# Adding twelve tiles of layer 0's expert outputs, where six were, beside its last four blocks

## The chip, the cores and the metric

The kernel runs on one core of a Trainium2 chip, as one launch. The metric is the device time of that core in microseconds (us). TensorE (PE) multiplies, PEld is its weight load, VectorE (DVE) does elementwise work and statistics, ScalarE (ACT) the activation functions and copies, GpSimd (POOL) the scatters with indices, and SyncE (SP) issues most of the loads.

## The reference: two layers of graph aggregation and experts

There are 3327 nodes with 256 features, `x`, and a sparse weighted adjacency `adj`. Each of two layers does the following, with a layernorm without parameters, `ln`, ahead of each half:

```
layer 0   x = x + relu(adj @ (ln(x) @ W) + b)
          x = x + sum over the 2 best of 8 experts, weighted:
                  relu(ln(x) @ W1[e] + b1[e]) @ W2[e] + b2[e]      (hidden size 1024)
layer 1   A = tanh(max(adj,0)^2)  kept to the 700 largest of each row
          x = x + relu(A @ (tanh(ln(x) @ Wp + bp) @ Wg) + bg)
          x = x + ln(x) + sum over the 2 best of 8 experts, weighted: (hidden size 256, gelu)
```

In both layers the two experts of a node are those with the largest scores of a linear router on `ln(x)`, and their weights are a softmax over the two scores. All arithmetic is in 32-bit floats. In the inputs no row of `adj` has more than 700 positive entries, so nothing is dropped in layer 1.

## The kernel before: tiles, panels, blocks, and the passage between the layers

**Tiles and panels.** The nodes are padded to 3328, which is 26 tiles of 128. `x` and a second array of the same size, `s`, stay in SBUF as 26 tiles of 256 columns. An aggregation (`aggregate`, line 326) goes through 13 panels of 256 nodes; for each panel two chunks of the adjacency are loaded into a ring of six places of 128x3328 numbers (`ring`, line 124), and TensorE multiplies them with all 26 tiles of `s` (line 340). `s` is only read there, so it is free while the experts run.

**Blocks.** The router lists each node's features under its two experts in `xlist0` in HBM. An expert's rows are then worked off in blocks of 256 rows (`experts`, line 700). One `step` (line 858) loads a later block's tokens, weights and biases through SP (lines 752 to 774, five loads, into two places of the ring, up to three blocks ahead), transposes the next block's tokens (line 785, copied by DVE in line 788), runs the first product (line 797, activation in line 804) and the second (line 839), adds the bias and multiplies by the weight on DVE (lines 846 and 847), and scatters the rows to their nodes' places in `ys0` in HBM with two indirect stores of GpSimd (line 464). A node has two rows in `ys0`, one for each of its experts.

**The order of the blocks.** `late_order` (line 68) writes it out by hand. Layer 0 has 30 blocks that always run, steps 0 to 29: the first eight are full blocks that could be planned before the last panels were there, and four single blocks of 128 rows are mixed in (steps 12, 17, 22 and 27). The planning goes in tiers: the first block of every expert, then the second of every expert, then the rest. After step 7 the first tier has been scattered, after step 16 (`tiers_done`, line 882) the second as well.

**What is done early.** The outputs of the first tiles can be added to `x` before the last blocks are done, if all rows of these tiles lie in blocks that have been scattered. The function `usual` (line 632) counts the rows of the first tiles for each expert, compares them with the rows that the blocks cover, and gives a flag; all engines branch on it in line 1179. In the first arm, `load_outputs` (line 901, SP) brings `ys0` rows of the first `BEGUN` tiles into columns of `s`, `add_loaded` (line 913, DVE) adds a tile's two rows to `x`, and `statistics` (line 246, DVE) takes mean and variance and works out the reciprocal root in three Newton steps. The one block's tokens that are transposed across the branch are put into `s` too (the `place` of line 1025). In the other arm all of that comes after the last block.

**The passage between the layers** (`between`, line 1090). `turned_pairs` (line 1053) goes through groups of tiles, `FOURS`. For a group that was not begun it loads the outputs into ring place 5 or 4 in turn (line 902), adds them (line 916) and takes statistics (lines 254 to 266); then, for each pair of tiles, it normalizes (line 276, into one of three buffers `xn`), transposes (line 288) and copies (line 289). `second_features` (line 1073) multiplies by `Wp` (line 1079), takes tanh (line 1086, `h2T`), multiplies by `Wg` (line 296) and copies the result into `s` (line 299). The loads of outputs of the groups not begun wait for all scatters. The first two panels of layer 1's matrix are filtered here as well (`filter_behind`, line 1113): DVE takes the maximum with 0 (line 1117), ScalarE the square and tanh in four pieces (lines 1120 and 1121). The first of these chunks stands on DVE behind the normalization of the last group but one, the others behind that of the last group. Then `aggregate` starts for layer 1.

**What sets the order.** [...] A scheduler places the instructions by its own estimates and priorities; `behind` (line 204) and `issue_after` pin an instruction behind another one.

Of the kernel before, what the change touches and what calls it, by code (L numbers as in the profile page):

```python
# [10 lines left out]
F32 = mybir.dt.float32  # L11
BF16 = mybir.dt.bfloat16
I32 = mybir.dt.int32
# [9 lines left out]
P = 128  # L23
NT = 26
NP = NT * P
D = 256
DC = D // P
E = 8
# [7 lines left out]
TOPK = 700  # L36
# [3 lines left out]
K = 2  # L40
# [18 lines left out]
EARLY = 8  # L59
# [5 lines left out]
FIXED = (4, 6)  # L65
# [9 lines left out]
    return order + list(range(LATE_PAIRS + fixed, LATE))  # L75


BEGUN, FIRST_TILES = 6, 14
FREE_PAN = NPAN - RING // NCHUNK
assert K * EARLY_PAN * PW >= E * (SB - 1) + EARLY * SB  # L80
PAIRS = [(t, 2) for t in range(0, NT, 2)]
FOURS = [(0, 2)] + [(t, 4) for t in range(2, NT, 4)]


@with_exitstack
def gnn_moe_two_layers(
# [24 lines left out]
    nc = tc.nc  # L111
# [3 lines left out]
    work = ctx.enter_context(tc.tile_pool(name="work", bufs=3))  # L115
# [5 lines left out]
    x = state.tile([P, NT, D], F32, name="x")  # L121
# [5 lines left out]
    for t in range(0, NT, 4):  # L127
        n = min(4, NT - t)
# [13 lines left out]
        out=before,  # L142
        in_=before,
# [53 lines left out]
    rows_written, early_rows, outputs, last_product, last_y = [], [], [], [], []  # L197
# [6 lines left out]
    def behind(instructions):  # L204

        if instructions and any(i is instructions[-1].ins for i in nc.cur_bb.bb.instructions):
            return tc.issue_after(instructions[-1].ins)
        return nullcontext()
# [37 lines left out]
    def statistics(t0, n, kept=None):  # L246


        st = work.tile([P, n, 6], F32, name="ln_st")
        mv, guess = kept or (  # L250
            work.tile([P, n, 2], F32, name="ln_mv"), work.tile([P, n], I32, name="ln_guess")
        )
        for g in range(n):
            nc.vector.bn_stats(out=st[:, g, :], in_=x[:, t0 + g, :])  # L254
            nc.vector.bn_aggr(out=mv[:, g, :], in_=st[:, g, :])
        ve = work.tile([P, n], F32, name="ln_ve")
        nc.vector.tensor_scalar(ve, mv[:, :, 1], EPS, None, ALU.add)  # L257
        half = work.tile([P, n], I32, name="ln_half")
        nc.vector.tensor_scalar(half, ve.bitcast(I32), 1, None, ALU.logical_shift_right)
        nc.vector.tensor_scalar(guess, half, -1.0, float(0x5F3759DF), ALU.mult, ALU.add)  # L260
        rs = guess.bitcast(F32)
        nw = work.tile([P, n], F32, name="ln_nw")
        for _ in range(3):
            nc.vector.scalar_tensor_tensor(nw, rs, -0.5, rs, ALU.mult, ALU.mult)
            nc.vector.tensor_tensor(nw, nw, ve, ALU.mult)
            nc.vector.scalar_tensor_tensor(rs, nw, 1.5, rs, ALU.add, ALU.mult)
        return mv, rs
# [83 lines left out]
    def rows_of(a, t0, n):  # L351
        return a[t0 * P : (t0 + n) * P, :].rearrange("(n p) d -> p n d", p=P)
# [279 lines left out]
    def usual(tiles, rows_, small):  # L632


        cnt = tokens(tiles, "pl_first_cnt")
        nc.vector.tensor_tensor(cnt, cnt, rows_, ALU.is_gt)
        most = work.tile([P, 1], F32, name="pl_most", bufs=1)
        nc.vector.tensor_reduce(most, cnt, AX.X, ALU.max)
        nc.vector.tensor_scalar(most, most, -1.0, 1.0, ALU.mult, ALU.add)
        for number, limit in small:  # L640
            nc.vector.scalar_tensor_tensor(
                most[0:1, :], number, float(limit), most[0:1, :], ALU.is_le, ALU.mult
            )
        flag = work.tile([P, 1], I32, name="pl_flag", bufs=1)
        nc.vector.tensor_copy(flag, most)
        return nc.values_load(flag[0:1, 0:1], min_val=0, max_val=1)
# [266 lines left out]
    def add_loaded(yt, t0, n):  # L913
        x_t = x[:, t0 : t0 + n, :]
        for k in range(K):
            nc.vector.tensor_tensor(x_t, x_t, yt[:, :, k * D : (k + 1) * D], ALU.add)  # L916
# [40 lines left out]
    def count(pan, chunks):  # L957
# [9 lines left out]
    layer0 = experts(  # L967
        xlist0, ys0, "0", FIXED[0], H, AF.Relu, f0_w1T, f0_b1, f0_w2T, f0_b2,
        nc.vector.tensor_copy,
    )  # L970
# [27 lines left out]
    with tc.issue_after(last_product[0].ins):  # L998
# [13 lines left out]
    most_all = const.tile([1, 1], F32, name="most_all")  # L1012
# [4 lines left out]
    most_int = const.tile([1, 1], I32, name="most_int")  # L1017
    nc.vector.tensor_copy(most_int, most_all)
    late = plan(positive.rearrange("p n i k -> p (n i k)"))
    layer0.steps_to(late, EARLY)  # L1020
    written = list(outputs)
    layer0.steps_to(late, layer0.always - 4)
    in_s = s.rearrange("p n d -> p (n d)")
    at = BEGUN * K * D
    layer0.step(late, place=in_s[:, at : at + DC * SB].rearrange("p (c b) -> p c b", c=DC))
# [3 lines left out]


    first_usual = usual(
        BEGUN, late[4][:, 0:E], [(late[5][0:1, :], FIXED[0]), (most_all, TOPK + 0.5)]
    )
    before_branch, rows_before = layer0.state(), list(rows_written)
    begun_stats = (
        const.tile([P, BEGUN, 2], F32, name="begun_mv"), const.tile([P, BEGUN], I32, name="begun_rs")
    )
    begun = []
    for t, n in FOURS:
        if t < BEGUN:  # L1040
            yt = in_s[:, 0 : n * K * D] if not begun else in_s[:, 2 * K * D : (2 + n) * K * D]
            begun.append((yt.rearrange("p (n d) -> p n d", n=n), t, n))

    def begin():
        for b in begun:
            add_loaded(*b)
        return statistics(0, BEGUN, begun_stats)


    ahead = RING // NCHUNK - 1  # L1050
# [2 lines left out]
    def turned_pairs():  # L1053


        for i, (t0, n0) in enumerate(FOURS):

# [67 lines left out]
    def new_layer1():  # L1125
        return experts(
            xlist1, ys1, "1", FIXED[1], D, AF.Gelu, f1_w1, f1_b1, f1_w2, f1_b2,
            nc.scalar.copy, kept=(EARLY // 2, w2_all, gate),
        )
# [47 lines left out]
            nc.scalar.dma_start(out=rows_of(out, t, n), in_=x[:, t : t + n, :])  # L1177

    with tc.If(first_usual > 0) as arms:
        layer0.step(late)  # L1180
        output_loads.clear()
        for yt, t, n in begun:
            load_outputs(yt, ys0, t, n, written, "read0")
        layer0.step(late)
        with behind(last_y):
            begin()
        layer0.steps_to(late, layer0.always)
        between()
        layer1 = new_layer1()
        aggregate(gnn_b_sb, filter_chunk, panels1(layer1), loaded=ahead)  # L1190
        late1 = first_blocks(layer1)


        layer1.steps_to(late1, layer1.tiers_done)
        written = list(outputs)
        layer1.step(late1, place=blk.tile([P, DC, SB], F32, name="xT_arms", bufs=1))
        second_usual = usual(FIRST_TILES, late1[4][:, E:], [(late1[5][0:1, :], FIXED[1])])
        before_inner = layer1.state()
        with tc.If(second_usual > 0) as inner:
            first_tiles = [(t, 2) for t in range(0, FIRST_TILES, 2)]  # L1200
            yts = [
                ring[i % RING][:, PIECE - 2 * K * D :].rearrange("p (n d) -> p n d", n=2)
                for i in range(len(first_tiles))
            ]
            k = 0
            while len(layer1.started) < layer1.always:
                layer1.step(late1)
                if k < len(first_tiles):
                    load_outputs(yts[k], ys1, *first_tiles[k], written, "read1")
                with behind(last_y):  # L1210
                    if 0 <= k - 2 < len(first_tiles):
                        add_loaded(yts[k - 2], *first_tiles[k - 2])
                if 0 <= k - 3 < len(first_tiles):
                    t, n = first_tiles[k - 3]
                    nc.sync.dma_start(out=rows_of(out, t, n), in_=x[:, t : t + n, :])
                k += 1
            assert k - 3 >= len(first_tiles)
            finish([(t, 2) for t in range(FIRST_TILES, NT, 2)])
        with inner.Else():
            layer1.back_to(before_inner)  # L1220
            layer1.rest(late1)
            finish(FOURS)
    with arms.Else():
        layer0.back_to(before_branch)
        rows_written[:] = rows_before
        layer0.rest(late)
        output_loads.clear()
        for yt, t, n in begun:
            load_outputs(yt, ys0, t, n, outputs)
        begin()  # L1230
        between()
        layer1 = new_layer1()
        most_reg = nc.values_load(most_int[0:1, 0:1], min_val=0, max_val=NP * GROUP)
        with tc.If(most_reg > TOPK) as many:
            with tc.tile_pool(name="topk", bufs=1) as tk:
                topk_rows(tc, tk, ring, psy, pst, adj, s, x, gnn_b_sb, ident, filtered, add_relu)
            for pan in range(NPAN):
                panels1(layer1)(pan)
        with many.Else():

            layer1.loaded.clear()
            first_arm = list(rows_written)
            rows_written.clear()
            aggregate(gnn_b_sb, filter_chunk, panels1(layer1), loaded=ahead)
        rows_written.extend(first_arm)
        early_rows.extend(first_arm)
        layer1.rest(first_blocks(layer1))
        finish(FOURS)

# [140 lines left out]
```

## Time and profile before

| what | value |
|---|---|
| median of 3 runs | 1262.3 us (1259.44 to 1262.47) |
| the profiled execution | 1255.26 us |
| its span in the trace | 1253.5 us |
| granted TensorE clock, mean | 0.989 |
| busy: PE / PEld / DVE / ACT / POOL | 96% / 83% / 57% / 41% / 23% |
| layer 0's aggregation ends, layer 1's starts | about 340 us, 805 us |
| layer 0's last four blocks, steps 26 to 29 | start 694.2, 708.2, 716.1 and 730.4 us, end 744.2 us |
| layer 1's aggregation ends | about 1099 us |

Times within the execution are counted from the start of its span. The profile's rows name an engine, a line of the code, the operation and the tiles that it writes and reads, with a count; a number in brackets is how long the engine sat idle before it, and what ended that. A matmul of 32-bit floats with 256 columns appears as two records. "SPq" is the queue in which SP issues its loads. Matmul rows in a timeline [...]overlap a little; the chain of waits gives the time from issue to issue.

### The profile page before, as it was taken

Reading aid. Unit: us, or ns where it says so; the run is one execution under the profiler, and the core shown is the slowest. Engines: PE = TensorE matmul, PEld = TensorE weight load, DVE = VectorE, ACT = ScalarE, POOL = GpSimd, SP = SyncE. Lnnn points to the kernel's source line nnn. Section 1 sums busy time; section 2 is a strip of 40 time slices with the busy share of each in tenths; the row PEclk is TensorE's granted clock in tenths of the full one; section 3 lists DMA queues with packets and bytes.
Section 4 is the critical chain, followed back from the end, with each engine's and each line's share of the span. In section 5 each row is a group of like instructions: output and inputs, shape, how many; then the busy total and the mean of one; then the engine's idle time right before and its main releaser. Section 6 shows DMA issues by size and latency. Waiting matters only on the chain.

```text
span 1253.5 us, 18523 instructions
## 1 busy us (share of the span) xinstructions
PE 1201.3 (96%) x5816; PEld 1035.3 (83%) x5816; DVE 712.2 (57%) x2919; ACT 519.3 (41%) x963; POOL 289.7 (23%) x363
## 2 busy tenths in 40 slices
PE   6999999999999999999999998999999999999992
PEld 5888888888888888888888887788888888877771
DVE  8267767677663111111111148668999998784454
ACT  3797455541022222323232234995455552043330
POOL 2023122131231111111111110302323223264432
PEclk9999999999999999999999998999999999999996
DMA  9676554454267655757566557244445542477696
GB/s 365 170 248 215 181 181 165 160 198 139 63 228 238 207 178 177 257 173 247 186 224 210 181 203 266 94 164 166 168 171 198 179 147 82 130 243 220 204 272 213
DMA packets 119546, 241.60 MB, mean 193 GB/s; under 512 B 21568, under 2 KB 89936, under 8 KB 112400
## 3 DMA queue, kind: packets, MB, share of 16 engines
q1 hardware_dynamic: 106624, 206.91, 50.3%
q0 software_dynamic: 11184, 31.85, 6.9%
q10 hardware_dynamic: 1632, 1.57, 0.4%
q8 instruction: 48, 0.79, 0.3%
q14 instruction: 58, 0.48, 0.1%
HBM read 203.99 MB, written 36.33 MB: 192 GB/s over the span
## 4 chain that ended last, share of the span: by engine, by line
PE 90%; DMA 4%; DVE 2%; issue 2%; ACT 1%; POOL 0%; SPq 0%; DVEq 0%; ACTq 0%; POOLq 0%
PE ps_g L340 47%; PE ps_y L839 18%; PE ps_h L797 18%; PE ps_s L296 4%; DMA ys<-wide,index 2%; DMA ring<-ys 2%; PE ptb L785 2%; PE ps_p L1079 1%; PE pt L288 1%; DVE x L916 0%; ACT xnT L289 0%; DMA x<-in_x 0%; DVE wide L846 0%; DVE ln_st L254 0%; POOL ys L464 0%
## 5 line engine op out<-in xcount | busy, mean ns | idle before, releaser
L340 PE MATMUL ps_g<-s,ring 128*128 128x256 f32 x2704 | 588.3, 380 | 0.0
L340 PEld LDWEIGHTS ps_g<-s,ring 128*128 128x128 f32 x2704 | 512.0, 190 | 68.7
L797 PE MATMUL ps_h<-xT,ring 128*128 128x256 f32 (+1 forms) x1176 | 252.6, 368 | 1.9 <-DVE xT L788 1.1
L797 PEld LDWEIGHTS ps_h<-xT,ring 128*128 128x128 f32 x1176 | 206.4, 190 | 39.7 <-ACT wide L804 4.7
L804 ACT ACTIVATE wide<-ps_h,ring 128x256 f32<-128x256 f32 (+1 forms) x240 | 110.1, 459 | 286.3 <-PE ps_h L797 278.1
L360 DVE SCALAR_TENSOR_TENSOR rt_product<-xn,gate 128x256 f32<-128x256 f32 x400 | 197.7, 494 | 12.4
L839 PE MATMUL ps_y<-ring,wide 128*128 128x256 f32 x896 | 200.3, 379 | 0.0
L464 POOL DMA_INDIRECT xlist<-xn,rt_idx x104 | 106.6, 1025 | 377.2 <-DVE ln_ve L257 301.7
L839 PEld LDWEIGHTS ps_y<-ring,wide 128*128 128x128 f32 x896 | 167.1, 190 | 21.0
L962 ACT ACTIVATE sign<-ring,below 128x416 bf16<-128x416 f32 x208 | 133.5, 642 | 72.6 <-DMA ring<-in_adjT 66.5
L464 POOL DMA_INDIRECT ys<-narrow,index x56 | 54.5, 972 | 331.4 <-DVE narrow L847 239.3
L788 DVE COPY xT<-ptb 128x512 f32<-128x512 f32 (+1 forms) x29 | 19.2, 663 | 153.5 <-PE ptb L785 153.5
L1110 ACT ACTIVATE ring<-ring 128x3328 f32<-128x3328 f32 x22 | 65.5, 2982 | 90.2 <-PE ps_g L340 37.2
L846 DVE TENSOR_TENSOR narrow<-ps_y,ring 128x256 f32<-128x256 f32 x56 | 23.8, 424 | 134.2 <-PE ps_y L839 132.7
L304 DVE TENSOR_TENSOR gnn_t<-ps_g,gnn_b_sb 128x256 f32<-128x256 f32 x52 | 21.9, 422 | 109.0 <-PE ps_g L340 96.3
L464 POOL DMA_INDIRECT ys<-wide,index x58 | 55.9, 965 | 63.4 <-DVE wide L847 40.3
L1111 ACT ACTIVATE ring<-ring 128x3328 f32<-128x3328 f32 x22 | 65.5, 2982 | 0.6
L804 ACT ACTIVATE narrow<-ps_h,ring 128x256 f32<-128x256 f32 (+1 forms) x64 | 28.9, 453 | 73.2 <-PE ps_h L797 54.7
L839 PE MATMUL ps_y<-s,narrow 128*128 x200 | 49.9, 390 | 5.5 <-issue 3.2
L425 ACT ACTIVATE rt_d<-rt_d 128x2 f32<-128x2 f32 x26 | 5.3, 202 | 115.2 <-DVE rt_d L424 115.2
L916 DVE TENSOR_TENSOR x<-x,ring 128x512 f32<-128x512 f32 (+1 forms) x36 | 30.2, 839 | 32.4 <-DMA ring<-ys 32.0
L839 PEld LDWEIGHTS ps_y<-s,narrow 128*128 128x128 f32 x200 | 35.4, 189 | 14.6 <-issue 8.6
(195 smaller groups left out, 1021.0 us busy)
## 6 DMA issues: line engine op xcount, KB each, us to landing
ring<-in_adjT SPq DMA_DIRECT2D x52, 1664.0 KB, 7.0
ring<-in_f_w1T SPq DMA_DIRECT2D x30, 1024.0 KB, 5.9
ring<-in_f_w2T SPq DMA_DIRECT2D x30, 1024.0 KB, 8.1
ring<-xlist SPq DMA_DIRECT2D x52, 258.0 KB, 2.9
ring<-in_f_w SPq DMA_DIRECT2D x36, 256.0 KB, 3.5
ring<-ys SPq DMA_DIRECT2D x13, 512.0 KB, 5.0
ring<-ys SPq DMA_DIRECT2D x5, 1024.0 KB, 5.5
ring<-in_f_b SPq DMA_DIRECT2D x34, 128.0 KB, 7.2
```

What stands on the lines that cost most here:

```text
L296: nc.tensor.matmul(ps, lhsT=lhsT[:, c, :], rhs=w_sb[:, c, :], start=(c == 0), stop=(c == DC - 1))
L340: nc.tensor.matmul(ps[it], lhsT=chunks[k][:, c, ts(it, P)], rhs=s[:, j, :], start=(j == 0), stop=(j == NT - 1),)
L360: nc.vector.scalar_tensor_tensor(product, xn[:, g, 0, 0:D], 1.0, gate[:, e, :], ALU.mult, ALU.mult, accum_out=sc[:, g, e : e + 1],)
L464: d = nc.gpsimd.indirect_dma_start(out=a[:, :], out_offset=bass.IndirectOffsetOnAxis(ap=index, axis=0), in_=rows_, in_offset=None,)
L785: nc.tensor.transpose(pt[:, c, ts(g, P)], xb[:, g, ts(c, P)], ident)
L797: nc.tensor.matmul(ps, lhsT=w1[:, c, ts(hc, P)], rhs=xT[:, c, :], start=(c == 0), stop=(c == DC - 1),)
L804: nc.scalar.activation(hT[:, hc, :], ps, func, bias=bb1[:, hc : hc + 1])
L839: last_product[:] = [nc.tensor.matmul(ps, lhsT=hT[:, hc, ts(g, P)], rhs=w2[:, hc, :], start=(hc == 0), stop=(hc == hc_n - 1),)]
L916: nc.vector.tensor_tensor(x_t, x_t, yt[:, :, k * D : (k + 1) * D], ALU.add)
L962: nc.scalar.activation(sign, a[:, :, ts(i, GROUP)], AF.Sign, bias=below, accum_out=positive[:, pan, i, k : k + 1],)
L1110: nc.scalar.activation(a, a, AF.Square)
L1111: nc.scalar.activation(a, a, AF.Tanh)
```

## The change: twelve tiles are begun instead of six

The first arm now begins 12 tiles, in three groups of four. Their rows must lie in the first two blocks of each expert, so `usual` compares with the rows that both tiers cover (`late[4][:, E:]`), and the loads wait for the outputs scattered by step 16 rather than by step 7. The branch is taken one step earlier, behind step 25. In the first arm the loads stand ahead of step 26; the adds stand behind step 27's last product on DVE, the statistics behind step 28's; before, the loads stood behind step 27's own loads, and adds and statistics both behind step 28's last product. `FOURS` no longer starts with a pair: it is six groups of four and a pair at the end, so that four groups (12, 16, 20 and 24 on) are left to the passage where five were. `statistics` takes a small buffer for each tile instead of one for each group, and lets two intermediate results share one; that gives room for twelve tiles. The columns of `s` are filled to the end: 12 tiles of outputs and the one block's tokens take all 26x256.

```diff
-BEGUN, FIRST_TILES = 6, 14
+BEGUN, FIRST_TILES = 12, 14
...
-FOURS = [(0, 2)] + [(t, 4) for t in range(2, NT, 4)]
+FOURS = [(t, min(4, NT - t)) for t in range(0, NT, 4)]
...
-        st = work.tile([P, n, 6], F32, name="ln_st")
...
         for g in range(n):
-            nc.vector.bn_stats(out=st[:, g, :], in_=x[:, t0 + g, :])
-            nc.vector.bn_aggr(out=mv[:, g, :], in_=st[:, g, :])
+            st = work.tile([P, 6], F32, name="ln_st")
+            nc.vector.bn_stats(out=st, in_=x[:, t0 + g, :])
+            nc.vector.bn_aggr(out=mv[:, g, :], in_=st)
...
-        half = work.tile([P, n], I32, name="ln_half")
+        nw = work.tile([P, n], F32, name="ln_nw")
+        half = nw.bitcast(I32)
...
-        nw = work.tile([P, n], F32, name="ln_nw")
...
-    layer0.steps_to(late, EARLY)
+    layer0.steps_to(late, layer0.tiers_done)
     written = list(outputs)
-    layer0.steps_to(late, layer0.always - 4)
+    layer0.steps_to(late, layer0.always - 5)
...
     first_usual = usual(
-        BEGUN, late[4][:, 0:E], [(late[5][0:1, :], FIXED[0]), (most_all, TOPK + 0.5)]
+        BEGUN, late[4][:, E:], [(late[5][0:1, :], FIXED[0]), (most_all, TOPK + 0.5)]
     )
...
-            yt = in_s[:, 0 : n * K * D] if not begun else in_s[:, 2 * K * D : (2 + n) * K * D]
+            yt = in_s[:, t * K * D : (t + n) * K * D]
...
-    def begin():
+    def add_begun():
         for b in begun:
             add_loaded(*b)
-        return statistics(0, BEGUN, begun_stats)
...
     with tc.If(first_usual > 0) as arms:
-        layer0.step(late)
         output_loads.clear()
         for yt, t, n in begun:
             load_outputs(yt, ys0, t, n, written, "read0")
         layer0.step(late)
+        layer0.step(late)
         with behind(last_y):
-            begin()
+            add_begun()
+        layer0.step(late)
+        with behind(last_y):
+            statistics(0, BEGUN, begun_stats)
         layer0.steps_to(late, layer0.always)
         between()
```

More of the change, by code (lines that the diff above doesn't have):

```diff
@@ L1229, in gnn_moe_two_layers @@
             load_outputs(yt, ys0, t, n, outputs)
-        begin()
+        add_begun()
+        statistics(0, BEGUN, begun_stats)
         between()
```

## The prediction, made before the changed kernel had run

> **What bounds the kernel now.** I read first the page's chain, then TensorE's timeline around the change, then the engines that TensorE waits for there.
>
> ```profile
> PE 90%; DMA 4%; DVE 2%; issue 2%; ACT 1%; POOL 0%; SPq 0%; DVEq 0%; ACTq 0%; POOLq 0%
> ```
>
> TensorE sets the time; only what shortens a wait of TensorE counts. The change touches the passage from layer 0's last blocks (up to 744.2) to layer 1's aggregation (from 805.2). There, by stage (us, then busy us of PE, PEld, DVE, ACT, POOL, clock, DMA share, GB/s):
>
> ```profile
> 756.40:760.90 4.50, 0.03 (x2) 0.05 (x1) 3.98 (x22) 0.37 (x1) 0.00 (x0) 0.75 0.99 403
> 760.90:766.00 5.10, 5.10 (x17) 4.29 (x18) 5.00 (x14) 1.65 (x3) 0.00 (x0) 0.55 1.05 421
> 766.00:789.00 23.00, 22.89 (x118) 19.22 (x117) 20.98 (x70) 12.99 (x29) 0.65 (x1) 1.00 0.47 166
> 789.00:805.20 16.20, 15.34 (x71) 12.01 (x70) 15.41 (x31) 15.84 (x29) 10.09 (x2) 1.00 0.28 106
> ```
>
> TensorE stands still for 4.5 us, then runs at half clock, then works at DVE's pace, and in the last 16 us ScalarE is full (15.84 of 16.20). TensorE's own rows (start, us, idle before it in brackets):
>
> ```profile
> 754.49 1.92 PE L296 MATMUL ps_s<-g_wg_sb,h2T 128*128 128x256 f32 x8
> 760.88 1.94 PE L288 MATMUL pt<-ident,xn 128*128 128x128 f32 x8 [4.47 <-DVE xn L276]
> 762.64 3.38 PE L1079 MATMUL ps_p<-xnT,proj_sb 128*128 128x256 f32 x8
> 790.50 1.99 PE L296 MATMUL ps_s<-g_wg_sb,h2T 128*128 128x256 f32 x8 [0.54 <-ACT h2T L1086]
> 805.23 7.07 PE L340 MATMUL ps_g<-s,ring 128*128 128x256 f32 x32
> ```
>
> The three pairs of tiles that were ready need 3.90 us each (transposes 0.44, L1079 1.73, L296 1.73); then the seventh tile is missing. Thirteen pairs are 50.7 us of work; the passage takes 805.2-744.2 = 61.0. What TensorE waits for, on DVE and then ScalarE:
>
> ```profile
> 753.56 2.49 DVE L916 TENSOR_TENSOR x<-x,ring 128x1024 f32<-128x1024 f32 x2 [8.50 <-DMA ring<-ys]
> 761.62 2.47 DVE L916 TENSOR_TENSOR x<-x,ring 128x1024 f32<-128x1024 f32 x2
> 769.67 2.48 DVE L916 TENSOR_TENSOR x<-x,ring 128x1024 f32<-128x1024 f32 x2
> ...
> 787.26 1.89 DVE L1117 TENSOR_SCALAR ring<-ring 128x3328 f32<-128x3328 f32 x1
> ```
>
> ```profile
> 789.19 0.90 ACT L1120 ACTIVATE ring<-ring 128x832 f32<-128x832 f32 x1 [0.28 <-DVE ring L1117]
> ...
> 803.56 0.51 ACT L1086 ACTIVATE h2T<-ps_p,g_bp_sb 128x256 f32<-128x256 f32 x1
> ```
>
> DVE can start on the late tiles only when they have landed (753.56) and takes 8.05 us for each four. Behind the fourth four and half of the last adds stands L1117 (787.26), the first filter of layer 1's matrix; behind that, on ScalarE, squares and tanhs (L1120, L1121) are mixed with the last pairs' work until the last h2T (803.56), which TensorE needs before it can aggregate. That list, not TensorE, sets 805.2.
>
> [...] after 4.47 us of idle, clock 0.55, and L1079's eight take 3.20 us in the chain instead of 1.73. [...] the 0.54 us at 790.50: h2T stood behind a filter piece. [...]
>
> **The change, part by part.** I also read the order of instructions in the built kernel.
>
> *The condition.* From the reference's inputs I worked out layer 0's routing: of the first 12 tiles' 3,072 rows no expert has more than 422, two blocks hold 512. So the first arm runs, as before (six tiles: 214 of 256).
>
> *The loads.* Before, two loads (0.5 and 1.0 MB) went out behind block 29's:
>
> ```profile
> SPq L902 <- DMA ys<-narrow,index: 32.5, 2, 24.7
> ```
>
> ```profile
> 695.05 0.39 SPq L752 DMA_DIRECT2D ring<-xlist  x1
> 709.10 0.38 SPq L752 DMA_DIRECT2D ring<-xlist  x1
> 720.92 0.89 SPq L902 DMA_DIRECT2D s<-ys  x2
> ```
>
> L902 also waited for the latest scatter of outputs: it issued at 720.92, 3.97 us after step 27's last product on DVE (716.95). Now three loads of 1.05 MB stand ahead of block 28's five on SP, and wait for step 25's scatter: 695.02+3.97 = 699.0, so block 28 goes from 695.05 to about 700.5. Its w1 is needed when step 28 starts, 716.1. By then 3.15+0.26+1.05 = 4.46 MB must come in 16 us, 279 GB/s. The DMA view moved 2.50 MB of block loads in 7.8 us (320 GB/s), and s and adjT loads at some 390: 3.15/0.39+1.31/0.32 = 12.2 us from 700.1, 712.3. Tokens come at about 709 for transposes at 713.5, w2 at 715.6 for 723.5. Block 29 keeps its time, set by block 26's end (709.1). Cost nothing, margin 3.8 us; if the cover goes, every us past 716.1 is on the path.
>
> *The adds.* 6 of 1.24 us instead of 3.56 in all: 7.4 us from 716.9, under step 28's 14.3 us of TensorE. Queued behind them is the copy of block 29's tokens: from 724.5 for 730.4. Nothing.
>
> *The statistics.* 12x0.39 and 12 small operations of 0.20, 7.1 us from 731.2, and six normalizations of 0.33: done at 741, under step 29. Nothing. One normalization now stands ahead of block 29's last product on DVE: the last scatter, and the loads of the late tiles, are 0.45 us later.
>
> *The branch* moves ahead of step 26. Step 27, first behind it now, took 7.87 us against 7.78 for the other single blocks: within 0.1 us, either sign. The smaller st and the shared nw leave DVE's order elsewhere as it was: nothing.
>
> *The passage.* Six pairs are ready instead of three, so TensorE has work from 744.2 to pair 8's L1079: transposes and start 1.25, eight pairs 31.2, L1079 1.73, to 778.4. The stall of 4.5 us and the half clock behind it go. What is late next: DVE's late tiles start at 753.56+0.45 = 754.0, three fours instead of four: 3x8.05 to 778.15, one add of 512 columns 0.65, L1117 1.89, so ScalarE's list starts at 780.75: 8.45 us earlier than 789.19. But in the built order it starts two pairs earlier in the work: pair 8's h2T stands behind the first filter piece. Up to the last h2T it now holds 14 filter pieces for 11, 9 h2T for 7, 8 copies to s for 6, 3 xnT for 2. With the spacings in ScalarE's full stretch (0.79, 0.37, 0.33, 0.49): before 8.69+2.59+1.98+0.98 = 14.2, from 789.19 803.4 (the trace: 803.56); after 18.5, from 780.75 799.2. Gain 8.45-4.26 = 4.2 us.
>
> *The new stall.* TensorE waits from 778.5 to about 782 for pair 8's h2T: 3.5 us, no further cost with the clock up, as TensorE is not last there. If the clock falls as after the 4.47 us (2.5 us lost over 16 matmuls), the next h2T come later, 1 to 2 us of it on the list. Gaps of 2.3 us at 1146 and 1162 cost under 0.5. I take 0.2 and keep 2.0. Sum: -4.2+0.2 = **-4.0 us**. The aggregation behind it is TensorE's own (22.55 us a panel without a wait) and passes this on in full.
>
> The profiled execution took 1255.26 us, 1253.5 its span: that becomes 1251.3. The median of the runs shown is 1262.3; the same 4.0 us give **1258.3**.
>
> **The rivals.** (1) *TensorE becomes the bound*: 744.2+50.7+1.2 = 796.1, gain 9, 1253.3. The stage sums speak for it; against it ScalarE's fixed order behind L1117. (2) *Half clock and a late landing eat it*: gain 0 to 3.5, about 1260.5; for it the new stall's length, against it that TensorE has slack there. (3) *The loads hold up block 28*: ahead of it 3.15 MB; decisive below 279 GB/s. At 175 (w1's page row: 1 MB in 5.9 us) w1 lands at 700.1+25.5 = 725.6, 9.5 us late, net +5.5: 1267.8, slower. Against it, the 320 and 390 in this very stretch. (4) *The branch isn't taken*: excluded by the counts.
>
> **How the numbers follow.** A measurement of this kernel can tell about 0.3% (3.8 us) from no change. The forecast's case, gain 3.8 to 5: 0.52. Rival 1: 0.09. Rival 2, with all gains under 3.8: 0.32. Rival 3 and other losses: 0.07. So faster 0.61, same 0.32, slower 0.07. The range reaches from just above rival 1 to gains of 0.8: 1253.6 to 1261.5.
>
> **What would show it.** In the new profile: no wait of TensorE for L276 in the passage, but one of some 3.5 us at pair 8's L296 for h2T; L1117 first at about 779; the aggregation's start 4 us earlier relative to 744.2; L902's loads on SP at 699 ahead of block 28's; no gap at step 28's start. A gap there, or a first L1117 near 787, or more than 1 us of low clock at 782, would make the prediction wrong.

## The result, and the profile after

The changed kernel takes 1257.88 us (median of 10 runs, 1256.38 to 1260.18) against 1262.38 us of the kernel before (10 runs, 1259.44 to 1263.58): a ratio of 0.9966, 95% interval 0.9958 to 0.9975, which is a gain of 4.5 us, with an interval of 3.2 to 5.3. The forecast was 1258.3 us and a gain of 4.0 us.

The two profiled executions can't be compared by their spans: 1253.5 us before, 1256.2 us after. From the start of layer 1's aggregation to the end, the execution of before took 448.3 us (1253.5-805.23), that of after 454.8, and those of the eleven experiments 454 to 459. So the profile of before is unusually short behind the passage. Only the passage itself is compared here: from TensorE's first transpose of the passage (L288) to the first long row of the aggregation (L340). Some lines of the code have another number now: L1078, L1085, L1116, L1119 and L1120 were L1079, L1086, L1117, L1120 and L1121.

TensorE after (start, duration in us, engine, line, what; in brackets the idle time before it):

```profile
743.66 0.60 PE L288 MATMUL pt<-ident,xn 128*128 128x128 f32 x4
...
778.08 0.27 PE L288 MATMUL pt<-ident,xn 128*128 128x128 f32 x1
781.29 2.08 PE L296 MATMUL ps_s<-g_wg_sb,h2T 128*128 128x256 f32 x4 [2.94 <-ACT h2T L1085]
...
801.45 1.89 PE L340 MATMUL ps_g<-s,ring 128*128 128x256 f32 x8
```

The wait of 4.47 us for L276 is gone; the new one of 2.94 us stands at the ninth pair's L296 and is for ScalarE's h2T. The passage takes 801.45-743.66 = 57.8 us instead of 805.23-744.04 = 61.2: 3.4 us less in these two executions, inside the interval of the medians. The same stretch by stage (us, then busy us of PE, PEld, DVE, ACT, POOL, clock, DMA share, GB/s):

```profile
743.70:778.00 34.30, 34.06 (x177) 28.93 (x176) 25.77 (x87) 19.29 (x42) 0.96 (x1) 1.00 0.68 259
778.00:782.50 4.50, 1.56 (x6) 1.04 (x5) 4.29 (x12) 2.53 (x5) 0.00 (x0) 0.84 0.32 62
782.50:788.00 5.50, 5.50 (x25) 4.40 (x24) 5.15 (x12) 3.99 (x9) 2.69 (x1) 0.82 0.64 269
788.00:801.40 13.40, 13.03 (x61) 10.66 (x60) 5.77 (x4) 13.32 (x26) 5.95 (x2) 1.00 0.00 1
```

TensorE is full until 778. Its granted clock is 0.50 from 781.1 to 784.5, behind the stall, and 1.00 after it (in the kernel before 0.50 from 758.7 to 765.5, then 1.00). In the last stage ScalarE is full (13.32 of 13.40). ScalarE's list begins, is held up once and ends with the last h2T here:

```profile
779.97 0.90 ACT L1119 ACTIVATE ring<-ring 128x832 f32<-128x832 f32 x1 [2.79 <-DVE ring L1116]
...
784.68 0.37 ACT L299 COPY s<-ps_s 128x256 f32<-128x256 f32 x1 [1.51 <-PE ps_s L296]
...
799.80 0.48 ACT L1085 ACTIVATE h2T<-ps_p,g_bp_sb 128x256 f32<-128x256 f32 x1
```

SP's loads in the stretch where the change begins:

```profile
699.01 1.48 SPq L902 DMA_DIRECT2D s<-ys  x3
701.97 0.39 SPq L752 DMA_DIRECT2D ring<-xlist  x1
...
704.58 6.04 SPq L774 DMA_DIRECT2D ring<-in_f_b  x1
712.37 0.39 SPq L752 DMA_DIRECT2D ring<-xlist  x1
```

### The profile page after: what moved, and what is told of

The parts are those of the page before. It is cut to its first block, busy times and chain, and to the rows that moved or that the text cites. A ratio compares the mean times of both kernels' runs of the same rounds, so it can differ in the third digit from the quotient of the medians.

```text
span 1256.2 us, 18512 instructions
## 1 busy us (share of the span) xinstructions
PE 1201.9 (96%) x5816; PEld 1035.6 (82%) x5816; DVE 711.2 (57%) x2907; ACT 518.6 (41%) x963; POOL 288.5 (23%) x363
## 4 chain that ended last, share of the span: by engine, by line
PE 88%; DVE 4%; DMA 3%; ACT 2%; issue 2%; POOL 1%; another core or an unknown queue 0%; POOLq 0%; DVEq 0%; ACTq 0%; SPq 0%
PE ps_g L340 47%; PE ps_y L839 19%; PE ps_h L797 18%; PE ps_s L296 2%; DMA ring<-ys 2%; PE ptb L785 2%; DVE x L916 1%; DMA ys<-wide,index 1%; DVE ln_st L254 1%; POOL ys L464 1%; DVE xn L276 1%; ACT xnT L289 0%; PE pt L288 0%; ACT ring L1120 0%
## 5 line engine op out<-in xcount | busy, mean ns | idle before, releaser
L340 PE MATMUL ps_g<-s,ring 128*128 128x256 f32 x2704 | 588.3, 380 | 0.0
L340 PEld LDWEIGHTS ps_g<-s,ring 128*128 128x128 f32 x2704 | 512.0, 190 | 68.7
L839 PE MATMUL ps_y<-ring,wide 128*128 128x256 f32 x896 | 200.3, 379 | 0.0
L839 PEld LDWEIGHTS ps_y<-ring,wide 128*128 128x128 f32 x896 | 167.1, 190 | 21.0
L839 PE MATMUL ps_y<-s,narrow 128*128 x200 | 51.2, 396 | 5.8 <-issue 2.0
L839 PEld LDWEIGHTS ps_y<-s,narrow 128*128 128x128 f32 x200 | 35.9, 192 | 15.3 <-issue 7.2
L254 DVE BATCH_NORM_STATS2 ln_st<-x 128x6 f32<-128x256 f32 x104 | 43.0, 420 | 4.8 <-DMA x<-in_x 3.7
```

Of the source, the lines that this page charges most:

```text
L254: nc.vector.bn_stats(out=st, in_=x[:, t0 + g, :])
L340: nc.tensor.matmul(ps[it], lhsT=chunks[k][:, c, ts(it, P)], rhs=s[:, j, :], start=(j == 0), stop=(j == NT - 1),)
L839: last_product[:] = [nc.tensor.matmul(ps, lhsT=hT[:, hc, ts(g, P)], rhs=w2[:, hc, :], start=(hc == 0), stop=(hc == hc_n - 1),)]
```

## The experiments

Three theories of what sets the end of the passage were told apart. **A**, the prediction's: ScalarE's queue, from its first filter piece to the last h2T. **B**: what counts is that TensorE's early stall of 4.5 us, and the half clock behind it, were removed. **C**, formed after the first four runs: in the kernel before it is DVE's late tiles, with TensorE's last two pairs behind them. All measured differences are against the kernel before, run beside each experiment; passages and ends come from each run's trace.

| run | passage, us | last L276 ends | time, us | against before | ratio, 95% |
|---|---|---|---|---|---|
| before | 61.2 | 795.95 | | | |
| the change | 57.8 | 784.77 | 1257.88 | -4.5 | 0.9958 to 0.9975 |
| place6 | 60.6 | 795.11 | 1261.26 | -0.9 | 0.9985 to 1.0007 |
| begun4 | 66.2 | 800.44 | 1267.48 | +5.3 | 1.0023 to 1.0053 |
| begun8 | 56.5 | 792.75 | 1257.00 | -5.2 | 0.9938 to 0.9969 |
| filters_last | 53.3 | 784.89 | 1255.08 | -7.1 | 0.9929 to 0.9957 |
| before_filters_last | 61.9 | 795.57 | 1262.67 | +0.3 | 0.9995 to 1.0011 |
| begun8_filters_last | 58.4 | 793.20 | 1260.47 | -1.9 | 0.9977 to 0.9990 |
| before_filter_behind | 60.9 | 793.34 | 1262.80 | +0.2 | 0.9989 to 1.0010 |
| pair8_first | 54.1 | 784.79 | 1255.57 | -6.8 | 0.9932 to 0.9958 |
| pair10_first | 52.8 | 784.50 | 1253.64 | -9.0 | 0.9914 to 0.9947 |
| loads2 | 60.3, begun 8.0 later | 796.95 | 1269.15 | +6.5 | 1.0035 to 1.0067 |
| loads3 | 59.7, begun 14.2 later | 803.57 | 1277.77 | +15.4 | 1.0102 to 1.0135 |

In all rows but the last two, the change of the passage and that of the time agree within 1.1 us: what the passage gains, the kernel gains.

### place6: the new place, the old six tiles

```diff
-BEGUN, FIRST_TILES = 12, 14
+BEGUN, FIRST_TILES = 6, 14
-FOURS = [(t, min(4, NT - t)) for t in range(0, NT, 4)]
+FOURS = [(0, 2)] + [(t, 4) for t in range(2, NT, 4)]
```

> The changed kernel with the six tiles and the groups of the kernel before: the branch one block earlier, the condition with two blocks, the loads ahead of block 28's, the adds beside step 28 and the small edits of the statistics stay. If the tiles make the gain (theories A and B) this equals the kernel before: -1.2 to +0.5 us. If the place makes it (the branch ahead of step 26, the loads earlier), -3 to -5 us.

Measured: -0.9 us, interval -1.9 to +0.9. The branch one step earlier, the loads ahead of block 28's, the split of adds and statistics and the small edits of the buffers together give nothing that can be told from zero. This run also takes back the new grouping, which ends with two tiles where the old one ends with four. The next two runs keep the new grouping, with four and eight tiles; halfway between their +5.3 and -5.2 us is +0.1, an estimate for six tiles in the new grouping. So the gain is that of the tiles, and, as far as this estimate goes, not that of the grouping.

### begun4 and begun8: how many tiles

```diff
-BEGUN, FIRST_TILES = 12, 14
+BEGUN, FIRST_TILES = 4, 14
```

begun8 has 8 in the same place.

> Four tiles are begun early. Two pairs of tiles are ready at 744 (7.8 us of TensorE), and five fours are late. Theory A (ScalarE's queue) expects the first filter 8.05 us later than before, at about 795, and the aggregation at 811: +5 to +6.5 us. Theory B (only TensorE's early stall counts) expects the stall to grow by one pair less, 3.9 us: +3.5 to +4.5 us.

> Eight tiles are begun early instead of twelve; all else as in the changed kernel. Four fours stay late, so the first filter on DVE (L1116) should again come at about 787, as in the kernel before (787.26), not at 778. Theory A as the prediction put it loosely (the first filter 8.45 us earlier is where the gain comes from) expects little: 0 to -1 us against before. Theory A read strictly (ScalarE's queue, counted from its first filter piece to the last h2T) has to count what is queued there: with no early stall TensorE is further on, so that fewer h2T and copies are left behind the first piece; it expects the aggregation at 800 to 801.5, -4 to -5 us against before, like the changed kernel. Theory B (what went is the stall of 4.5 us and the half clock behind it, wherever the filter stands) expects -4 to -7 us.

begun4 lost 5.3 us (2.9 to 6.7): A's range, while B's lies within the interval too. begun8 gained as much as the change itself with two thirds of the tiles, though its first filter stood at 786.04 on DVE, nearly as late as before (787.26). So the loose form of A, that the earlier first filter is the gain, fell. Its strict form and B both fit: the aggregation starts at 800.18, and TensorE has an early stall of only 1.45 us and no low clock (1.00 from 743.7 to 800.2). The end of DVE's work and the start of the aggregation in begun8:

```profile
792.01 0.74 DVE L276 TENSOR_SCALAR xn<-x,ln_mv,ln_guess 128x256 f32<-128x256 f32 x2
```

```profile
800.18 3.19 PE L340 MATMUL ps_g<-s,ring 128*128 128x256 f32 x14
```

From the end of the last L276, 792.75, to the aggregation it is 7.4 us; in the kernel before and in place6, where four tiles come last and not two, it is 9.28 us. In the change it is 16.7 us: there DVE is done long before. That led to C. It is only a hint: begun4 also ends with two tiles and takes 9.33 us, since TensorE waits there for ScalarE and reaches the last pair late, at 801.40:

```profile
799.57 1.99 PE L296 MATMUL ps_s<-g_wg_sb,h2T 128*128 128x256 f32 x8 [0.86 <-ACT h2T L1085]
```

### filters_last: the change with ScalarE's filters behind the last h2T

```diff
-            nc.scalar.activation(h2T[:, oc, :], ps, AF.Tanh, ...)
+            last_h2T[:] = [nc.scalar.activation(h2T[:, oc, :], ps, AF.Tanh, ...)]
...
             nc.vector.tensor_scalar(a, a, 0.0, None, ALU.max)
+        with tc.issue_after(last_h2T[0].ins):
             for q in range(4):
```

The third panel's square and tanh are pinned in the same way.

> The changed kernel with all squares and tanhs of layer 1's first panels put behind the last h2T on ScalarE; DVE's part of the filters stays. Theory A (ScalarE's queue sets the start of the aggregation) expects the stall of 2.9 us at 781 gone, the last h2T at about 791, and the aggregation at 797 to 798.5, held by the first chunk's pieces of 6.4 us: 3 to 4 us less than the changed kernel, -6.5 to -8.5 us against before, if the later filters still come in time. If TensorE or DVE sets it by now, nothing changes against the changed kernel (-4 to -5 us); if the pieces behind come too late, it is slower than that.

Measured: -7.1 us, the passage 4.5 us shorter than the change's. Its stages, the first filter's wait left out:

```profile
743.70:778.00 34.30, 34.06 (x178) 28.84 (x175) 25.62 (x87) 19.72 (x43) 0.96 (x1) 1.00 0.69 261
778.00:795.40 17.40, 17.35 (x86) 14.33 (x84) 15.34 (x26) 10.36 (x23) 0.38 (x2) 1.00 0.27 99
```

```profile
797.05 25.30 PE L340 MATMUL ps_g<-s,ring 128*128 128x256 f32 x116 [1.71 <-ACT ring L1125]
```

TensorE now works without a gap to 795.34, 51.6 us for its 13 pairs; then it waits 1.71 us for the first filter pieces (L1125 here). In the changed kernel ScalarE's queue did set the end, both by the stall that it causes and by its length: A is right there.

### before_filters_last and begun8_filters_last: the same edit where fewer tiles are begun

The diff is that of filters_last, made on the kernel before and on begun8.

> The kernel before (six tiles) with the squares and tanhs of layer 1's first panels put behind the last h2T on ScalarE, as in the run filters_last; DVE's part of the filters stays where it was. Theory A, as the prediction put it (in the kernel before ScalarE's queue, not TensorE, sets 805.2), expects the aggregation as early as TensorE's own work with its stall and half clock allows, 50.7+1.2+7 us after 744.2, 803.1, or earlier: -2 us or more. Theory C (in the kernel before it is DVE's late tiles: the last normalization ends at 795.95, and two pairs of TensorE's work, 7.8 us and 1.5 to start, follow it) expects nothing from it: 804.5 to 806.5, -0.7 to +1.3 us.

> Eight tiles begun, and all squares and tanhs behind the last h2T. Theory A expects that clearing ScalarE helps here as it helped with twelve tiles: the aggregation near 797, -7 to -8 us against before. Theory C expects that DVE's late tiles hold it (in the run begun8 the last normalization ended at 792.75 and the aggregation began 7.4 us later), so that clearing ScalarE gives nothing, and the first chunk's pieces, now begun only behind the last h2T, cost 1.7 us and more: 800.2 to 803.2, -2 to -5 us against before, and 0 to 3 us slower than begun8.

The edit that gave the changed kernel 2.6 us more gives the kernel before nothing (+0.3) and costs the one with eight tiles 3.3 us (-5.2 to -1.9). C expected that, A the opposite. In begun8_filters_last TensorE still waits for the last normalization:

```profile
793.03 0.67 PE L288 MATMUL pt<-ident,xn 128*128 128x128 f32 x4 [0.69 <-DVE xn L276]
```

It is done 7.5 us after the end of that normalization (793.20 to 800.67), as in begun8, and then waits 1.71 us for the first filter pieces. TensorE in before_filters_last:

```profile
794.75 0.41 PE L288 MATMUL pt<-ident,xn 128*128 128x128 f32 x2 [0.79 <-DVE xn L276]
805.49 29.84 PE L340 MATMUL ps_g<-s,ring 128*128 128x256 f32 x137 [1.71 <-ACT ring L1126]
```

Nothing of ScalarE's filters stands in the way, and still TensorE is done only at 803.78 (805.49-1.71): it waits for DVE's last normalizations, and two pairs follow. From the last L276 that is 8.2 us instead of 9.28, so the filters in ScalarE's queue were worth some 1.1 us of the kernel before, and the wait of 1.71 us, which the edit itself brings, eats that.

### before_filter_behind: the kernel before with its first filter taken out of DVE's way

```diff
-        with tc.issue_after(normal[-2 if pan == 0 and k == 0 else -1].ins):
+        with tc.issue_after(normal[-1].ins):
```

> The kernel before with one edit: its first filter on DVE (L1117, 1.89 us), which stands ahead of the last four normalizations, is put behind them. Theory C (DVE's late tiles set the aggregation's start in the kernel before) expects the last normalization to end 1.8 us earlier, at 794.1, and the aggregation at 803.4 to 804: -1.2 to -2 us. Theory A (ScalarE's queue from its first piece sets it, and here the first piece is pushed from 789.19 to about 796) expects a later start: +1 us or more.

Measured: +0.2 us, interval -1.4 to +1.3, between the two expectations. DVE's last normalizations in the kernel before, and here:

```profile
794.57 1.38 DVE L276 TENSOR_SCALAR xn<-x,ln_mv,ln_guess 128x256 f32<-128x256 f32 x4
```

```profile
791.96 1.38 DVE L276 TENSOR_SCALAR xn<-x,ln_mv,ln_guess 128x256 f32<-128x256 f32 x4
```

Counted from the passage's start the last one ends 1.9 us earlier, and the passage is only 0.3 us shorter. From that normalization it now takes 10.9 us: the first pieces, from 795.30, stand between the last pairs' h2T on ScalarE, and TensorE waits for one of these:

```profile
798.17 1.99 PE L296 MATMUL ps_s<-g_wg_sb,h2T 128*128 128x256 f32 x8 [0.57 <-ACT h2T L1086]
```

So in the kernel before two limits lie within 2 us of each other: lifting DVE's alone meets ScalarE's, lifting ScalarE's alone meets DVE's. Lifting both at six tiles wasn't tried. A third limit is near as well: TensorE's own 51.6 us (filters_last), its early stall of 4.47 and the 2.4 us that it lost at half clock (L288 and L1079 took 4.97 us, from 760.88 to 765.85, for work of 2.6) make 58.4 of the 61.2 us, an estimate. So an edit of DVE's or ScalarE's order behind the stall can win at most 2.8 us with six tiles; the shorter passages of the change and of begun8 need the stall gone. By this estimate B has a part in the gain too.

### pair8_first and pair10_first: the new stall taken away

```diff
         with tc.issue_after(normal[-2 if first else -1].ins):
             nc.vector.tensor_scalar(a, a, 0.0, None, ALU.max)
+        with tc.issue_after((h2T_of[16] if first else normal[-1]).ins):
             for q in range(4):
```

`first` is the first chunk of panel 0, and `h2T_of` holds each pair's last tanh. In pair10_first the added line is

```diff
+        with tc.issue_after(h2T_of[20 if first else NT - 2].ins):
```

and the third panel's square and tanh also wait for the last h2T.

> The changed kernel with one edit of order: the first chunk's squares and tanhs on ScalarE wait for the h2T of the ninth pair (tile 16), which stood behind the first piece. The prediction held that TensorE has slack in the stall of 2.94 us at 781 and that the half clock costs 0.2 us: then this gives -0.7 us (two h2T fewer behind the list's start) to 0 against the changed kernel, -4.5 to -5.2 us against before. The rival (the stall, and the low clock that follows it until 788, hold up the h2T and copies that ScalarE's list waits for; ScalarE stood still for 1.51 us at 784.7) expects the aggregation at 797.5 to 799.5: 2 to 4 us less than the changed kernel, -6.5 to -8.5 us against before.

> The changed kernel with both lessons: the first chunk's squares and tanhs on ScalarE wait for the h2T of the eleventh pair (tile 20), all other pieces for the last h2T. No wait of TensorE should be left in the passage: from 743.7 its own 13 pairs with their start take 51.6 us (measured in filters_last), so the aggregation begins at 795.4 to 796.5, 1 us before filters_last: -8 to -9.5 us against before. If ScalarE or DVE still hold it, -6.5 to -7.5 us as in filters_last and pair8_first.

pair8_first is faster than before by 6.8 us, 2.3 more than the change; its passage is 3.7 us shorter than the change's. The stall became 1.47 us:

```profile
783.92 1.99 PE L296 MATMUL ps_s<-g_wg_sb,h2T 128*128 128x256 f32 x8 [1.47 <-ACT h2T L1085]
797.66 5.56 PE L340 MATMUL ps_g<-s,ring 128*128 128x256 f32 x25
```

Behind it the clock is 1.00 (782.5 to 799) and the eight L296 take 1.99 us, where four took 2.08 us behind the stall of 2.94 us. Not all of the gain is the stall's price, though. ScalarE's list starts at the same time (780.00) and takes 16.0 us to the last h2T (796.01) where the change needs 19.83. But it also holds two filter pieces and two h2T less up to there, which is 2.3 us with the spacings of the prediction; that leaves some 1.5 us for the stall and its half clock, an estimate. pair10_first took the rest of the stall away:

```profile
743.40:778.00 34.60, 34.36 (x178) 29.08 (x177) 26.01 (x88) 19.79 (x43) 0.97 (x1) 1.00 0.67 259
778.00:796.30 18.30, 17.81 (x88) 14.74 (x87) 14.94 (x25) 14.91 (x29) 0.55 (x2) 1.00 0.26 94
```

TensorE is busy 52.2 of 52.9 us: this is rival 1's case, TensorE as the bound, with the aggregation at 796.25 where the prediction had 796.1 for it. With -9.0 us it is the fastest version.

### loads2 and loads3: the cover of the early loads

```diff
         for yt, t, n in begun:
             load_outputs(yt, ys0, t, n, written, "read0")
+            load_outputs(yt, ys0, t, n, written, "read0")
```

loads3 has the added line twice.

> The changed kernel with each of the three early loads of outputs issued three times, to the same places: 9.4 MB instead of 3.15 MB at 699, five of the nine ahead of block 28's w1 in SP's order. If the prediction's margin is real and bounded (w1 at 712.3 with three loads, needed at 716.1, and 2.7 us for each further load), two further loads ahead make w1 1.6 us late and the tokens and the wait of one load for another add to it: step 28 starts 2 to 5 us later, and all behind it, -3 to +0.5 us against before. If loads ahead of block 28 cost nothing at any size, it equals the changed kernel: -4.5 us. If they cost as much as their bytes (6.3 MB, 16 us), some +10 us.

> The changed kernel with each of the three early loads issued twice, to the same places; five of the six go ahead of block 28's on SP, so two loads, 2.1 MB, more than in the changed kernel, which is 5.4 us at 390 GB/s, 6 us at the 350 that loads3 moved. To be read at the start of step 28 (715.56 in the changed kernel). If the margin of 3.8 us in the prediction was there, step 28 starts 1.5 to 2.5 us late. If w1 landed just in time in the changed kernel (loads3: four loads and 12.0 us more, 12.2 us late), it starts 4.5 to 6.5 us late. The total: what step 28 loses, less up to 3 us by another order on ScalarE in the passage.

Both cost far more than expected. In loads2 five loads went ahead of block 28's, in loads3 seven (not five, as the expectation had it). SP's queue and TensorE in loads2:

```profile
698.73 9.14 SPq L902 DMA_DIRECT2D s<-ys  x5
709.37 0.39 SPq L752 DMA_DIRECT2D ring<-xlist  x1
```

```profile
718.50 1.09 PE L785 MATMUL ptb<-ident,ring 128*128 128x128 f32 x4 [5.65 <-DMA ring<-xlist]
719.38 4.29 PE L839 MATMUL ps_y<-ring,wide 128*128 128x256 f32 x10
723.51 1.89 PE L797 MATMUL ps_h<-xT,ring 128*128 128x256 f32 x8
```

Not w1 but block 28's tokens came late: they kept step 27's second product waiting for 5.65 us, the half clock behind it (0.50 from 717 to 719, 0.56 in the mean from 719 to 724) added 2 us (L839's ten in 4.29 instead of 2.32), and step 28 began at 723.51 instead of 715.56, 8.0 us late, where 1.5 to 6.5 were expected. In loads3 the waits are 9.54 us for the tokens and 1.54 for w1, and step 28 begins 12.2 us late. Without more loads TensorE could begin on the tokens, by both runs, 5.7 to 6.1 us (two loads of 1.05 MB at 365 GB/s, the mean from 701 to 719 in loads2, or at 344, from 705 to 725 in loads3) and 12.2 us (four, at 344) earlier than 718.50 and 725.10: at 712.4 to 712.9, an estimate, for transposes that began at 712.96. A part of the delay can be the waits of the second copy for the first at the same place (SP's L902 waited three times for s<-ys from 695 to 725, 13.2 us in all); against much of it, the DMA engines were 0.91 to 1.08 busy from 701 to 719 in loads2. The changed kernel's own trace says much the same: its GB/s by stretches, added up from 699, reach the 3.41 MB that end with the tokens at 709.8; in loads2 they reach the 5.51 MB at 715.5, 3.0 us before TensorE began (718.50). The same 3.0 us give 712.8, an estimate. So in the changed kernel the tokens were in time by less than 1 us, by both estimates. Why loads3's time rose by 2.7 us more than its passage ended later was not pursued.

## Why the prediction was right, and where it was not

**The sum.** The forecast was -4.0 us, the medians give -4.5 (3.2 to 5.3). In the two traces the terms are: ScalarE's list starts 36.3 us into the passage instead of 45.2, 8.8 earlier (forecast 8.45), and takes 21.5 us to the aggregation instead of 16.0, 5.4 more (forecast 4.26 and 0.2). 8.8-5.4 = 3.4. The count of the list was exact: up to the last h2T the trace has 14 filter pieces, 9 other h2T, 8 copies to s and 3 xnT. The early stall went, as forecast.

**The term that was mis-sized is the new stall.** Its length was forecast as 3.5 us and was 2.94; its price was taken as 0.2 us. From the first filter piece to the last h2T the list took 19.83 us, and in it ScalarE stood still for 1.51 us at 784.68, for L296's products, which TensorE finished late at half clock (four in 2.08 us). In the kernel before it took 14.37 us, so that it grew by 5.46 us where the counts give 4.26: the price was 1.2 us, or 1.5 by pair8_first. The prediction named "more than 1 us of low clock at 782" as a sign that it is wrong. That sign came: the clock was 0.50 for 3.4 us. The number stayed close since the list began 0.4 us earlier than forecast; the 0.6 us left over (3.4 instead of 4.0) is less than the medians can tell.

The price rested on a misreading. The prediction says "Gaps of 2.3 us at 1146 and 1162 cost under 0.5". The chain of waits has pieces of 2.28 and 2.32 us there, named "issue". But TensorE's own rows show it at work, after 0.32 and 0.36 us of idle time:

```profile
1145.62 1.99 PE L839 MATMUL ps_y<-s,narrow 128*128 x8 [0.32 <-issue]
1161.46 1.99 PE L839 MATMUL ps_y<-s,narrow 128*128 x8 [0.36 <-issue]
```

The nearer row, the 4.47 us in the same passage, was kept for the range only. Here 2.94 us between two groups were followed by the half clock (0.50), and 1.47 us, in pair8_first, were not (1.00).

**The step that was wrong is "That list, not TensorE, sets 805.2", for the kernel before.** There DVE's late tiles set it as well: with the list out of the way TensorE still ended at 803.78, only 1.1 us earlier in the passage, and the kernel gained nothing. For the changed kernel the sentence holds (filters_last). That the difference of two lists came out right is in part luck: in the kernel before the limits end close together, so that the list's end was also the end of the others. With eight tiles the strict count of the list even hit the start of the aggregation (800 to 801.5 expected, 800.18 measured), and yet taking the list out of the way gained nothing there.

**The rest.** The condition held: the three loads of the first arm are in the trace. The loads issued at 699.01 (699.0), block 28's at 701.97 (700.5); block 29's came at 712.37, not at 709.1, as SP's issue of block 28's last load was held for 6.04 us; that cost nothing. "Cost nothing, margin 3.8 us" was right in its first half. The margin was hardly there, and it was the tokens', not w1's, that ran out first in loads2: the bytes ahead were divided by a rate, with no time for a load to be reported as landed. The trace of before had it, in the view of line 752 for blocks 28 and 29:

```profile
L752 SPq DMA_DIRECT2D ring<-xlist x2: 377/382/387, 695.1 to 709.1; - x2
...
DMA to landing us min/median/max: 2.9/2.9/2.9
```

The one landing in it is that of block 29's tokens: 258 KB, landed 2.9 us after their issue, and only 0.75 us of that are bytes at 350 GB/s (the view by slices has 345 to 361 at its fastest there). With the other 2.2 us added, the 709 of the prediction becomes 711.2, an estimate, and half of the 4.5 us of margin for the tokens is gone; by the estimates above less than 1 us was there. The adds took 7.0 us from 716.49 under step 28, the statistics and six normalizations from 730.76 to 740.25 under step 29 (forecast 741), and DVE began on the late tiles at 753.26 (forecast 754.0, with a passage 0.4 us earlier). Branch and buffers: nothing (place6).

**The rivals.** Rival 3's mechanism is real and was closer than its chance of 0.07 said: two more loads ahead turn the change into +6.5 us. Rival 1 was kept out by ScalarE's fixed order, as argued, and appears when that order is changed. Rival 2 was partly true: the new stall and its half clock cost some 1.5 us, but the measured gain, 4.5 us, is above the range of 0 to 3.5 that it gave.

## What to carry to other kernels

Several engines that end within two or three microseconds of each other are one joint limit: to learn which sets it, move one engine's work out of the way at a time, and expect a gain only when the last of them moves. A sum for one engine that comes out right doesn't show that this engine is the limit. A long piece of the chain of waits is not yet a gap: look at the engine's own rows. Where more work is made ready early, look at what is queued behind the first late piece on each engine (the first h2T behind ScalarE's first filter piece came 2.94 us late for TensorE); here, with twelve tiles, pinning ScalarE's filter pieces behind the work that TensorE waits for gave as much again as the whole change (pair10_first). Putting all of them behind the last h2T gave nothing with six tiles and cost 3.3 us with eight. A load put ahead of others needs the landing time of the others (here 2.9 us for 258 KB), not the bytes alone, before it counts as covered.

## What was not expected of the hardware

- TensorE's gap of 2.94 us in the change was followed by a clock of 0.50; those of 1.45 us (begun8) and 1.47 us (pair8_first) were not, the clock stayed at 1.00. In the profile after, a gap of 2.32 us that ended at 1121.16 was followed by 0.50 too, from 1122.4 to 1125.8, when TensorE was at work again.
- The clock was 0.50 for 3.4 us behind the gap of 2.94 us and for 3.4 us behind that of 2.32 us, and for 6.8 us in the kernel before (4.47 us of gap), where it began at 758.7, 2.3 us after TensorE had stopped. In loads3, behind 9.54 us and with 1.54 us more of gap in it, it was 0.57 in the mean from 720 to 725, 0.50 to 730 and 0.90 to 735. Gaps of nearly one length differ: behind 4.21 us in place6 the eight L288 took 1.33 us and the eight L1078 3.57; behind 4.23 us in before_filter_behind the same work took 1.94 and 3.78.
- With 3.15 MB of loads and block 28's behind each other in its queue, SP's issue of one load took 6.04 us (from 704.58) instead of 0.4; the load behind it, block 29's tokens, was issued at 712.37. Why that one was held isn't shown.
- The part behind the passage took 448.3 us in the profiled execution of before and 454 to 459 us in twelve others with the same work there, so that one profile's span says less than its stages.
